# Two batches' softmax in another order: the first one finished first, its transpose in halves, one power for both norms

## The chip, the cores and the metric

The kernel runs on one core of a Trainium2 chip. The metric is the device time of one execution in microseconds (us): the median of several runs. PE is the matrix engine (TensorE), PEld its weight loads, DVE the VectorE, ACT the ScalarE, POOL the GpSimd, SP the engine that issues nearly all DMAs.

## The reference

For 64 batches of 128 tokens and 512 features, x gets a residual added: multi-query attention with 16 heads of width 64, one key and one value shared by all heads, between two layernorms. All of it is fp32.

```python
xn = layernorm(x, g_in)
q = (xn @ Wq).reshape(b, n, H, DH).transpose(0, 2, 1, 3) * DH ** (-0.5)
kv = xn @ Wkv                       # k, v: 64 columns each, shared by the heads
# a null key and a null value (from cond) stand ahead of the 128 others
sim = einsum('bhid,bjd->bhij', q, k) + bias
sim = where(causal or masked, -max, sim)
attn = softmax(sim)
out = einsum('bhij,bjd->bhid', attn, v).reshape(b, n, H * DH) @ Wo
x = x + layernorm(out, g_out)
```

## The kernel before, in words

Every engine executes its instructions in the order in which the Python program issues them (a manual schedule); an instruction waits for the results, and for the buffers, that it needs. So the order of the calls in the step functions is the order on each engine, and there is no planner.

The 64 batches are handled as 32 pairs. Step `d` has a first part, `turn_full(d)`, and a second, `body_full(d)`; the steps 4 to 29 use these two, the first and last steps have functions of their own. In step `d` four jobs are under way at once:

- the **softmax** of the batches `a = 2d` and `b = 2d + 1`;
- the **output** of the pair before, `p = 2d - 2`: probabilities times values (`values`), then the product with Wo (`out_product`, seven products of a Strassen scheme, with sums of the inputs by `out_sum` on POOL);
- the **last norm** and the store of the pair before that, `l = 2d - 4`;
- for the group of four batches to come, `g = d // 2 + 1`: q, by an outer and an inner Strassen scheme (`product_two`, `inner_products` on PE, and `inner_out`, which adds inner products from PSUM into `qT` on DVE), k and v (`kv_pair`, `kv_pair_out`), and for the group after it the first norm of two batches `m` and `m + 1` of x.

A step with even `d` (`h = 0`, "even step" below) also has `token_sums_inner` on POOL; a step with odd `d` ("odd step") transposes the values (`values_T`) and starts the sums of the next group (`next_sums`, POOL).

The scores of a batch are an array `s` of 128 partitions by 8 rows by 194 columns. It has a lower part (`hf = 0`, 64 keys) and an upper part (`hf = 1`, 128 keys), each normalized by itself because the rows are different queries. Per batch and part:

- `scores_max`, DVE, L831: negative row maxima, `nmax`;
- `exps`, ACT, L840: one exponential for each of the 8 rows, with the row sum taken along (each has a second instruction that reads the accumulator);
- `rinv`, DVE, L858: reciprocals of the sums;
- `scale`, POOL, L862: the part times the reciprocals.

When both parts of a batch are scaled, `blocks_T` (DVE, L878) transposes the whole in blocks of 32 by 32 into `sb`, from which `values` reads in the next step. `bias_add` (POOL, L764) writes bias plus mask into the `s` of a coming batch. There are three buffers for `s`, so `bias_add(b + 2)` writes where batch `a` was and waits for the transpose of `a`.

The inner products of q have four outputs, `pi2`, `pi3`, `pi7` and `pi4` in the trace's names (the trace merges them as `pi`). Each takes seven small matmuls whose sums build up in three PSUM regions. PE may only overwrite or add to a region after DVE's `inner_out` (L744) has read its state: PE and DVE hand each other the same tile several times a step. `out_keep(p, "X", "yu2")` (DVE, L1055) is such a hand-over for the output product in `pyX`: it copies product 6's state before product 7 adds to it.

The norms: `two_stats` (L316 to L321) takes statistics of two tiles on DVE and a power of -1/2 on POOL (`pow`), and `two_nmr` (L327) makes -mean/std from them on DVE. `norm_apply` (ACT, L358) and `pair_norm` (ACT, L1092) apply the norm to x and to the output; `tokens_T` (L382) transposes the normalized x; `pair_gain` (L1095) and `pair_residual` (L1098) finish an output, `store` sends it.

Of the kernel before, what the change touches and what calls it, by code (L numbers as in the profile page):

```python
# [17 lines left out]
def kernel(  # L18
# [63 lines left out]
    P = 128  # L82
# [223 lines left out]
        nc.gpsimd.tensor_tensor(rstd, rstd, nhalf, ALU.pow)  # L306
        stats[m] = mv, rstd

    def two_stats(tiles, name):

        mv = small.tile([P, 2, 2], FP, tag=f"mv{name}", name=f"mv{name}")
        rstd = small.tile([P, 2], FP, tag=f"rs{name}", name=f"rs{name}")
        sts = []
        for t in tiles:
            st = small.tile([P, 6], FP, tag="st", name="st")
            nc.vector.bn_stats(st, t)  # L316
            sts.append(st)
        for i, st in enumerate(sts):
            nc.vector.bn_aggr(mv[:, i], st)
        nc.vector.tensor_scalar(rstd, mv[:, :, 1], EPS, None, ALU.add)  # L320
        nc.gpsimd.tensor_tensor(rstd, rstd, nhalf.broadcast_to([P, 2]), ALU.pow)  # L321
        return mv, rstd

    def two_nmr(mv, rstd, name):
        nmr = small.tile([P, 2], FP, tag=f"nm{name}", name=f"nm{name}")
        for i in range(2):
# [8 lines left out]
        return [(nmr[:, i : i + 1], rstd[:, i : i + 1]) for i in range(2)]  # L335

    xnmr = {}

# [812 lines left out]
    def turn_full(d):  # L1151

        a, b, p = 2 * d, 2 * d + 1, 2 * d - 2
        g, h = d // 2 + 1, d % 2
        home = lower_rooms(a)
        scores(a, 0, home=home[0])
        scores(b, 0, home=home[1])
        scores(a, 1)
        scores(b, 1, ((ps_y, "X"), (ps_q, "c")))
        scores_add(a, 0)  # L1160
        scores_add(b, 0)
        scores_max(a, 0)
# [12 lines left out]
        exps(a, 0)  # L1175
        keep_two("a", g, h, "p1")
        scores_max(b, 0)
        rinv(a, 0)
        scale(a, 0)
        exps(b, 0, 0, 3)  # L1180
        values_out(p, po)
        step_home(d)

    def next_sums(g):

        for k in (1, 2, 3):
            token_sum(g, k)
        token_sums_inner(g, 2)
# [255 lines left out]
    def body(d):  # L1444
# [20 lines left out]
        if h == 1:  # L1465
            load_mask(g + 1)
        if ln:
            nmrs[l], nmrs[l + 1] = two_nmr(*on, "o")
        xn = two_stats((xs[m], xs[m + 1]), "x")
        scores_max(a, 1)  # L1470
        product(g, f0, 1, ps_q, "a")
        keep("a", g, f0, "p1")
# [7 lines left out]
            product(g, f0, 2, ps_w, "w")  # L1480
            q_out(g, f0, 0, "w", "p1")
        scores_max(b, 1)
        xnmr[m], xnmr[m + 1] = two_nmr(*xn, "x")
        if ln:
            pair_gain(l)
            pair_residual(l)
# [105 lines left out]
    def body_full(d):  # L1592
# [3 lines left out]
        xw = g + 1 < NG  # L1596
        m = (g + 1) * GB + 2 * h
        sums = h == 0
        if sums:
            token_sums_inner(g, 7)  # L1600
        if xw:
            xn = two_stats((xs[m], xs[m + 1]), "x")
        on = two_stats((ys[l], ys[l + 1]), "o")
        pkv = kv_pair(g * GB + 2 * h, (ps_q, "c"))
        if xw:
            xnmr[m], xnmr[m + 1] = two_nmr(*xn, "x")
        nmrs[l], nmrs[l + 1] = two_nmr(*on, "o")
        scores_max(a, 1)
        kv_pair_out(g * GB + 2 * h, pkv)
        if h == 1 and xw:  # L1610
            load_mask(g + 1)
        if xw:
            norm_apply(m)
            norm_apply(m + 1)
        product_two(g, h, 6, ps_q, "a", start=False)
        inner_room(2, g, h)
        inner_products(2, g, h, (1,))
        out_sum(p, 0)
        if sums:
            token_sum(g, 4)  # L1620
        out_product(p, 1, ps_y, "X")
        out_sum(p, 1)
        out_sum(p, 2)
        if xw:
            tokens_T(m)
            tokens_T(m + 1)
            if h == 1:
                tokens_out(g + 1)
        pair_norm(l)
        inner_out(2, g, h, "00")  # L1630
        keep_two("a", g, h, "u2")
        scores_max(b, 1)
        out_keep(p, "X", "yp1")
        pair_norm(l + 1, (ps_y, "Y"))
        product_two(g, h, 5, ps_q, "c")
        exps(b, 0, 3)
        pair_gain(l)
        pair_residual(l)
        store(l)
        pair_gain(l + 1)  # L1640
        inner_products(2, g, h, (6,))
        inner_out(2, g, h, "01")
        if sums:
# [13 lines left out]
        if sums:  # L1657
            token_sums_inner(g, 4)
# [12 lines left out]
        out_product(p, 5, ps_y, "Y")  # L1671
        exps(a, 1, 2)
        if not sums:
            scale(b, 0)
        rinv(a, 1)
        scale(a, 1)
        if sums:
            scale(b, 0)
# [18 lines left out]
        if h == 1:  # L1697
            values_T(g)
# [213 lines left out]
```

## Time and profile before

| | |
|---|---|
| time, median of 3 runs | 1085.35 us (1085.19 to 1085.71) |
| the profiled execution: time / span | 1085.17 us / 1083.4 us |
| mean granted TensorE clock | 0.998 |
| busy, share of the span | PE 95%, PEld 83%, DVE 83%, POOL 74%, ACT 61% |
| HBM | 63.19 MB read, 33.55 MB written |

The time of the profiled execution is 1.8 us above its span; the rest of the text compares with this execution. How to read the rows:

- A timeline row has the start and the duration in us, the engine, the line and operation, `out<-in` by the program's names, the shape, the number of instructions merged (x2), and in brackets how long the engine had been idle and whose result ended that.
- A row of the waits reads "engine line <- engine line it waited for: us in total, times, longest us".
- A row of the stages has the window in us, its length, and the busy us (and instructions) of PE, PEld, DVE, ACT and POOL, then the granted clock, the DMA share and GB/s.
- A row of the groups has the number of instructions after x, then busy us and mean ns of one, then idle us before them.

### The profile page before, as it was taken

Reading aid. Unit: us, or ns where it says so; the run is one execution under the profiler, and the core shown is the slowest. Engines: PE = TensorE matmul, PEld = TensorE weight load, DVE = VectorE, ACT = ScalarE, POOL = GpSimd, SP = SyncE. Lnnn points to the kernel's source line nnn. Section 1 sums busy time; section 2 is a strip of 40 time slices with the busy share of each in tenths; the row PEclk is TensorE's granted clock in tenths of the full one; section 3 lists DMA queues with packets and bytes.
Section 4 is the critical chain, followed back from the end, with each engine's and each line's share of the span. In section 5 each row is a group of like instructions: output and inputs, shape, how many; then the busy total and the mean of one; then the engine's idle time right before and its main releaser. Section 6 shows DMA issues by size and latency. Waiting matters only on the chain.

```text
span 1083.4 us, 32419 instructions
## 1 busy us (share of the span) xinstructions
PE 1034.0 (95%) x12805; PEld 901.4 (83%) x12805; DVE 897.4 (83%) x1954; ACT 661.9 (61%) x2675; POOL 798.6 (74%) x676
## 2 busy tenths in 40 slices
PE   9999999999999999999999999999999999999997
PEld 8888878878888788888888888888887888888886
DVE  6867778888888888888888888888888888887787
ACT  4766657755567555676555775556765557745483
POOL 4998588596785967759677595776868768686676
PEclk9999999999999999999999999999999999999999
DMA  7415242421524215152241522415224152321211
GB/s 207 133 30 140 65 131 73 123 70 60 145 62 125 84 46 149 55 137 75 68 139 42 146 72 86 114 42 147 79 90 103 42 160 68 99 72 41 86 61 59
DMA packets 73839, 100.92 MB, mean 93 GB/s; under 512 B 32212, under 2 KB 36056, under 8 KB 71896
## 3 DMA queue, kind: packets, MB, share of 16 engines
q1 hardware_dynamic: 73392, 98.47, 30.8%
q8 instruction: 100, 1.64, 0.6%
q14 instruction: 51, 0.42, 0.1%
q10 hardware_dynamic: 296, 0.40, 0.1%
HBM read 63.19 MB, written 33.55 MB: 89 GB/s over the span
## 4 chain that ended last, share of the span: by engine, by line
PE 59%; POOL 22%; DVE 14%; issue 4%; ACT 1%; DMA 0%; POOLq 0%; DVEq 0%
PE pi L716 11%; PE pyX L1028 10%; PE pyY L1028 7%; POOL s L764 7%; PE pa L618 5%; POOL xS L561 4%; PE po L939 4%; PE pkv L419 3%; POOL xI L695 3%; POOL s L862 3%; DVE sb L878 3%; PE pyw L1028 3%; DVE qT L744 3%; PE pq L514 3%; DVE nmax L831 3%
## 5 line engine op out<-in xcount | busy, mean ns | idle before, releaser
L840 ACT ACTIVATE s<-s,nmax 128x65 f32<-128x65 f32 (+1 forms) x1024 | 371.2, 369 | 78.4 <-DVE nmax L831 78.3
L862 POOL TENSOR_TENSOR s<-s,rinv 128x512 f32<-128x512 f32 (+1 forms) x132 | 190.1, 1446 | 143.3 <-DVE rinv L858 143.0
L764 POOL TENSOR_TENSOR s<-biasp,mneg 128x1552 f32<-128x1552 f32 (+1 forms) x65 | 206.1, 3173 | 45.1 <-ACT mneg L751 39.9
L744 DVE TENSOR_TENSOR qT<-pi,qT 128x128 f32<-128x128 f32 (+1 forms) x480 | 161.1, 345 | 62.5 <-PE pi L716 57.1
L840 ACT ACTIVATION_READ_ACCUMULATOR s<-s,nmax 128x1 f32 x1024 | 197.8, 193 | 0.0
L1064 ACT COPY y<-pyX 128x256 f32<-128x256 f32 x29 | 10.8, 373 | 249.3 <-PE pyX L1028 249.3
L831 DVE TENSOR_REDUCE nmax<-s 128x8 f32<-128x1032 f32 (+1 forms) x128 | 121.8, 952 | 0.1
L878 DVE STREAM_TRANSPOSE sb<-s 128x1536 f32<-128x1536 f32 (+1 forms) x68 | 112.4, 1657 | 3.6 <-POOL s L862 3.6
L1028 PE MATMUL pyX<-wT,oT 128*128 128x256 f32 x464 | 109.8, 380 | 0.0
L1028 PE MATMUL pyX<-wo,oT 128*128 128x256 f32 x464 | 109.8, 380 | 0.0
L1008 POOL TENSOR_TENSOR oT<-oT 128x512 f32<-128x512 f32 x64 | 81.4, 1274 | 15.0 <-PE pyw L1028 12.8
L1028 PEld LDWEIGHTS pyX<-wT,oT 128*128 128x128 f32 x464 | 84.2, 191 | 9.1
L1028 PEld LDWEIGHTS pyX<-wo,oT 128*128 128x128 f32 x464 | 84.2, 191 | 9.0
L939 PE MATMUL po<-sb,vr 32*64 32x128 f32 (+1 forms) x3232 | 83.5, 301 | 0.5 <-DVE s L824 0.4
L939 PEld LDWEIGHTS po<-sb,vr 32*64 32x64 f32 x3232 | 71.6, 130 | 14.0 <-issue 9.1
L716 PE MATMUL pi<-xS,wq 128*128 128x128 f32 x260 | 55.6, 296 | 26.5 <-DVE qT L744 26.5
L716 PEld LDWEIGHTS pi<-xS,wq 128*128 128x128 f32 x260 | 41.2, 190 | 41.6 <-DVE qT L744 36.9
L939 PE MATMUL po_s<-sb,vr 32*64 32x128 f32 (+1 forms) x864 | 65.3, 302 | 1.0 <-DVE s L826 1.0
L419 PE MATMUL pkv<-xT,wkv 128*128 128x256 f32 x256 | 63.3, 391 | 0.0
L958 ACT ACTIVATE oT<-po,nv 128x512 f32<-128x512 f32 (+1 forms) x101 | 61.6, 654 | 0.6 <-POOL s L764 0.6
L1028 PE MATMUL pyY<-wo,oT 128*128 128x256 f32 x256 | 60.6, 380 | 0.0
L1028 PE MATMUL pyw<-wo,oT 128*128 128x256 f32 x256 | 60.5, 380 | 0.0
(243 smaller groups left out, 2690.7 us busy)
## 6 DMA issues: line engine op xcount, KB each, us to landing
out_dram<-y SPq DMA_DIRECT2D x63, 256.0 KB
x<-in_x_dram SPq DMA_DIRECT2D x62, 256.0 KB
xd<-xb SPq DMA_DIRECT2D x14, 1024.0 KB
xT<-xd SPq DMA_DIRECT2D x56, 256.0 KB
home<-in_x_dram SPq DMA_DIRECT2D x56, 256.0 KB
vr<-vd SPq DMA_DIRECT2D x64, 128.0 KB
kT<-kT SPq DMA_DIRECT2D x32, 64.0 KB
vd<-vb SPq DMA_DIRECT2D x32, 64.0 KB
```

The source lines that it names most:

```text
L419: nc.tensor.matmul(pkv, wkv[:, kc, :], xT[g][:, t : t + 2, kc, :], start=(kc == 0), stop=(kc == KC - 1),)
L716: nc.tensor.matmul(to, inner_w[k][i][:, h], inner_x[k, g][i], start=(i == 1), stop=True, skip_group_check=(i != 1),)
L744: nc.vector.tensor_tensor(o, p, o, ALU.add)
L764: nc.gpsimd.tensor_tensor(S[b][:, :, keys], biasp[:, :, keys], mneg[:, t, keys] .unsqueeze(1) .broadcast_to([P, R8, keys.stop - keys.start ...
L831: nc.vector.tensor_reduce(nmax[b][:, hf], S[b][:, :, WITH_NULL[hf]], AX.X, ALU.max, negate=True)
L840: nc.scalar.activation(row, row, AF.Exp, bias=nmax[b][:, hf, k : k + 1], accum_out=rsum[b][:, hf, k : k + 1],)
L862: nc.gpsimd.tensor_tensor(sv, sv, rinvs[b, hf][:, lo:hi].unsqueeze(2).broadcast_to([P, hi - lo, sv.shape[2]]), ALU.mult,)
L878: nc.vector.transpose(sbs[b][:, :, lo:hi].rearrange("p j e q -> p e j q"), S[b][:, lo:hi, 1 : ROW - 1].rearrange("p e (j k) -> p e j k", k=Q),
L939: nc.tensor.matmul(po[s][rows, to : to + n], vr[g][quad, t, PLACE[j], :], sb[quad, slots, r * NF : (r + 1) * NF, :], start=(turn == 0), st ...
L958: nc.scalar.activation(to, src, AF.Identity, bias=nv2)
L1008: eng.tensor_tensor(o, a, b, op)
L1028: nc.tensor.matmul(prod[key], h[:, c, :], w[:, c, :], start=(start and c == 0), stop=(c == HC - 1), skip_group_check=not start,)
```

## The change

Lines of the changed program are two to four higher than before for the same operation (L744 is L746, L862 is L864, L878 is L880). The change is in `body_full`, but for the norm helpers and one line of `turn_full` that concerns step 4 alone.

- **Exponentials.** Before: 5 lower ones of `b` (three were done in the first part of the step), 8 upper ones of `a`, 8 upper ones of `b`. Now: 8 upper ones of `a`, 5 lower of `b`, 8 upper of `b`. `rinv(a, 1)` and `scale(a, 1)` move ahead of `rinv(b, 0)` and `scale(b, 0)`.
- **Transposes.** `blocks_T(a)` and `blocks_T(b)` become two halves each (`lo`: rows 0 to 3, `hi`: rows 4 to 7). Those of `a` stand among the reads of `pi7`, `pi3` and `pi2`, ahead of where the whole one stood. Those of `b` stand ahead of and behind the last reads of `pi4`. `scale(b, 1)` is cut likewise.
- **`bias_add(b + 2)`** goes ahead of `scale(b, 1)` on POOL. In step 29 the one for the last batch goes with it.
- **Norms.** `stats_of` takes the four tiles (two of x, two of the output) in one go with one power, and `nmr_of` makes the four results after it; `scores_max(a, 1)` stands between.
- **Order on DVE besides.** `tokens_T`, the first read of `pi2` and the gains come earlier, `scores_max(b, 1)` and `values_T` later.

```diff
+    def stats_of(tiles, name):
+        n = len(tiles)
...
         nc.vector.tensor_scalar(rstd, mv[:, :, 1], EPS, None, ALU.add)
-        nc.gpsimd.tensor_tensor(rstd, rstd, nhalf.broadcast_to([P, 2]), ALU.pow)
+        nc.gpsimd.tensor_tensor(rstd, rstd, nhalf.broadcast_to([P, n]), ALU.pow)
...
     def turn_full(d):
         if d == 4:
-            next_sums(g)
+            token_sum(g, 1)
+            token_sum(g, 2)
...
     def body_full(d):
-        if xw:
-            xn = two_stats((xs[m], xs[m + 1]), "x")
-        on = two_stats((ys[l], ys[l + 1]), "o")
+        tiles = [ys[l], ys[l + 1]]
+        if xw:
+            tiles = [xs[m], xs[m + 1], *tiles]
+        n4 = stats_of(tiles, "n")
+        scores_max(a, 1)
         pkv = kv_pair(g * GB + 2 * h, (ps_q, "c"))
+        nm = nmr_of(*n4, "n")
...
-        scores_max(a, 1)
         kv_pair_out(g * GB + 2 * h, pkv)
...
-        scores_max(b, 1)
         out_keep(p, "X", "yp1")
-        exps(b, 0, 3)
...
         pair_gain(l + 1)
+        exps(a, 1)
         inner_products(2, g, h, (6,))
...
+        scores_max(b, 1)
         out_product(p, 2, ps_w, "w")
...
-        rinv(b, 0)
-        exps(a, 1, 0, 2)
         keep_two("a", g, h, "u3")
+        rinv(a, 1)
+        scale(a, 1)
         inner_products(2, g, h, (7, 5, 2))
         inner_out(2, g, h, "11")
         inner_out(2, g, h, "00,11")
+        exps(b, 0, 3)
...
+        rinv(b, 0)
+        scale(b, 0)
+        blocks_T(a, *lo)
         out_product(p, 5, ps_y, "Y")
-        exps(a, 1, 2)
...
+        exps(b, 1, 0, 2)
         inner_products(7, g, h, (6,))
         inner_out(7, g, h, "01")
+        out_keep(p, "Y", "yp5")
+        exps(b, 1, 2)
...
         q_out_two(g, h, 1, 1, "c", "u3")
+        blocks_T(a, *hi)
         inner_products(2, g, h, (4, 3))
         inner_out(2, g, h, "01,10")
-        exps(b, 1, 0, 4)
-        out_keep(p, "Y", "yp5")
-        exps(b, 1, 4)
+        bias_add(b + 2)
+        if d == PAIRS - 3:
+            bias_add(B - 1)
...
         rinv(b, 1)
-        blocks_T(a)
-        scale(b, 1)
-        bias_add(b + 2)
-        if d == PAIRS - 3:
-            bias_add(B - 1)
+        scale(b, 1, *lo)
+        scale(b, 1, *hi)
         if h == 1 and xw:
             next_sums(g + 1)
         inner_products(4, g, h, (6,))
         inner_out(4, g, h, "01")
+        if h == 1:
+            values_T(g)
         out_product(p, 7, ps_y, "X", start=False)
         out_part(p + 1, 1, "X")
+        blocks_T(b, *lo)
         inner_products(4, g, h, (7, 5, 2))
...
-        blocks_T(b)
+        blocks_T(b, *hi)
         out_product(p, 4, ps_y, "X", start=False)
```

PE's order and SP's order of DMAs stay as they were. The order on POOL in the odd step 15 (batches `a` = 30 and `b` = 31), from the output sums to the next group's sums, before:

```order
L1008 TENSOR_TENSOR oT_28_6557<-oT_28_6557 128x512 x2
L862 TENSOR_TENSOR s_31_6351<-s_31_6351,rinv_31_0_6667 128x8x64
L862 TENSOR_TENSOR s_30_6135<-s_30_6135,rinv_30_1_6698 128x8x128
L862 TENSOR_TENSOR s_31_6351<-s_31_6351,rinv_31_1_6748 128x8x128
L764 TENSOR_TENSOR s_33_6753<-biasp_86,mneg_118 128x1552
L561 TENSOR_TENSOR xS1_9_6755<-xT_9_6651 128x512
```

The same stretch of POOL now, where `s_33` is the buffer of `s_30`:

```order
L1010 TENSOR_TENSOR oT_28_6535<-oT_28_6535 128x512 x2
L864 TENSOR_TENSOR s_30_6115<-s_30_6115,rinv_30_1_6648 128x8x128
L864 TENSOR_TENSOR s_31_6310<-s_31_6310,rinv_31_0_6666 128x8x64
L766 TENSOR_TENSOR s_33_6700<-biasp_86,mneg_118 128x1552
L864 TENSOR_TENSOR s_31_6310<-s_31_6310,rinv_31_1_6716 128x4x128 x2
L563 TENSOR_TENSOR xS1_9_6720<-xT_9_6626 128x512
```

Batch 30 is scaled first, and the bias of batch 33 stands ahead of the last scaling of batch 31, which is in two. On DVE in the same step, the end from the last reciprocal on, before (`pi4` and `pyX` are PE's, `sb` the transposes):

```order
L858 RECIPROCAL rinv_31_1_6748<-rsum_31_6553 128x8
L878 STREAM_TRANSPOSE sb_30_6750<-s_30_6135 128x8x6x32
L744 TENSOR_TENSOR qT_8_1_0_6459<-pi4_8_1_6728,qT_8_1_0_6459 128x2x64
L1062 TENSOR_TENSOR y_29_6718<-pyX_28_1_6613,y_29_6718 128x256
L744 TENSOR_TENSOR qT_8_1_0_6459<-pi4_8_1_6728,qT_8_1_0_6459 128x2x64
L744 TENSOR_TENSOR qT_8_1_0_6459<-pi4_8_1_6728,qT_8_1_0_6459 128x2x2x64
L636 TENSOR_TENSOR qT_8_1_1_6460<-pc_8_1_5_6633,qT_8_1_1_6460 128x8x64
L1062 TENSOR_TENSOR y_28_6629<-pyY_28_5_6686,y_28_6629 128x256
L744 TENSOR_TENSOR qT_8_1_0_6459<-pi4_8_1_6728,qT_8_1_0_6459 128x4x64
L878 STREAM_TRANSPOSE sb_31_6786<-s_31_6351 128x8x6x32
```

The same end on DVE now:

```order
L860 RECIPROCAL rinv_31_1_6716<-rsum_31_6531 128x8
L746 TENSOR_TENSOR qT_8_1_0_6437<-pi4_8_1_6706,qT_8_1_0_6437 128x2x64
L459 STREAM_TRANSPOSE vb_8_6732<-vT_8_6176 64x512
L1064 TENSOR_TENSOR y_29_6680<-pyX_28_1_6591,y_29_6680 128x256
L880 STREAM_TRANSPOSE sb_31_6747<-s_31_6310 128x4x6x32
L746 TENSOR_TENSOR qT_8_1_0_6437<-pi4_8_1_6706,qT_8_1_0_6437 128x2x64
L746 TENSOR_TENSOR qT_8_1_0_6437<-pi4_8_1_6706,qT_8_1_0_6437 128x2x2x64
L638 TENSOR_TENSOR qT_8_1_1_6438<-pc_8_1_5_6606,qT_8_1_1_6438 128x8x64
L1064 TENSOR_TENSOR y_28_6601<-pyY_28_5_6671,y_28_6601 128x256
L746 TENSOR_TENSOR qT_8_1_0_6437<-pi4_8_1_6706,qT_8_1_0_6437 128x4x64
L880 STREAM_TRANSPOSE sb_31_6747<-s_31_6310 128x4x6x32
```

The transpose of batch 30 no longer stands between the last reciprocal and the second read of `pi4`; the first half of batch 31's now stands ahead of the third and fourth reads.

In the stretch of DVE before these, from the first reads of `pi3` to its last read, the order before was:

```order
L744 TENSOR_TENSOR qT_8_1_1_6460<-pi3_8_1_6683,qT_8_1_1_6460 128x2x64
L744 TENSOR_TENSOR qT_8_1_0_6459<-pi7_8_1_6671,qT_8_1_0_6459 128x4x64
L744 TENSOR_TENSOR qT_8_1_0_6459<-pi7_8_1_6671,qT_8_1_0_6459 128x2x2x64
L636 TENSOR_TENSOR qT_8_1_1_6460<-pc_8_1_5_6633,qT_8_1_0_6459 128x8x64
L744 TENSOR_TENSOR qT_8_1_0_6459<-pi2_8_1_6610,qT_8_1_0_6459 128x4x64
L744 TENSOR_TENSOR qT_8_1_0_6459<-pi4_8_1_6728,qT_8_1_0_6459 128x2x64
L1055 COPY y_28_6629<-pyX_28_1_6613 128x256
```

And now, with the first half of batch 30's transpose ahead of it:

```order
L860 RECIPROCAL rinv_31_0_6666<-rsum_31_6531 128x8
L880 STREAM_TRANSPOSE sb_30_6669<-s_30_6115 128x4x6x32
L746 TENSOR_TENSOR qT_8_1_0_6437<-pi7_8_1_6643,qT_8_1_0_6437 128x2x64
L746 TENSOR_TENSOR qT_8_1_1_6438<-pi3_8_1_6663,qT_8_1_1_6438 128x2x64
L746 TENSOR_TENSOR qT_8_1_0_6437<-pi7_8_1_6643,qT_8_1_0_6437 128x4x64
L746 TENSOR_TENSOR qT_8_1_0_6437<-pi7_8_1_6643,qT_8_1_0_6437 128x2x2x64
L638 TENSOR_TENSOR qT_8_1_1_6438<-pc_8_1_5_6606,qT_8_1_0_6437 128x8x64
L880 STREAM_TRANSPOSE sb_30_6669<-s_30_6115 128x4x6x32
L746 TENSOR_TENSOR qT_8_1_0_6437<-pi2_8_1_6587,qT_8_1_0_6437 128x4x64
L746 TENSOR_TENSOR qT_8_1_0_6437<-pi4_8_1_6706,qT_8_1_0_6437 128x2x64
L1057 COPY y_28_6601<-pyX_28_1_6591 128x256
```

Both halves of batch 30 now stand on DVE ahead of the first read of `pi4` and the copy from `pyX`.

More of the change, by code (lines that the diff above doesn't have):

```diff
@@ L320, in two_stats, with nmr_of @@
         nc.vector.tensor_scalar(rstd, mv[:, :, 1], EPS, None, ALU.add)
-        nc.gpsimd.tensor_tensor(rstd, rstd, nhalf.broadcast_to([P, 2]), ALU.pow)
+        nc.gpsimd.tensor_tensor(rstd, rstd, nhalf.broadcast_to([P, n]), ALU.pow)
         return mv, rstd
-    def two_nmr(mv, rstd, name):
-        nmr = small.tile([P, 2], FP, tag=f"nm{name}", name=f"nm{name}")
-        for i in range(2):
+    def nmr_of(mv, rstd, name):
+        n = rstd.shape[1]
+        nmr = small.tile([P, n], FP, tag=f"nm{name}", name=f"nm{name}")
+        for i in range(n):
             nc.vector.tensor_scalar(
@@ L334, in two_nmr @@
             )
-        return [(nmr[:, i : i + 1], rstd[:, i : i + 1]) for i in range(2)]
+        return [(nmr[:, i : i + 1], rstd[:, i : i + 1]) for i in range(n)]
     xnmr = {}
@@ L1598, in body_full @@
         sums = h == 0
[L1599 removed]
+        lo, hi = (0, R8 // 2), (R8 // 2, R8)
+        if d == 4:
+            token_sums_inner(g, 2)
+        elif sums:
             token_sums_inner(g, 7)
+        tiles = [ys[l], ys[l + 1]]
         if xw:
[L1602 to L1603 removed]
+            tiles = [xs[m], xs[m + 1], *tiles]
+        n4 = stats_of(tiles, "n")
+        scores_max(a, 1)
         pkv = kv_pair(g * GB + 2 * h, (ps_q, "c"))
+        nm = nmr_of(*n4, "n")
+        nmrs[l], nmrs[l + 1] = nm[-2:]
         if xw:
[L1606 to L1608 removed]
+            xnmr[m], xnmr[m + 1] = nm[:2]
         kv_pair_out(g * GB + 2 * h, pkv)
@@ L1617, in body_full @@
         inner_products(2, g, h, (1,))
+        inner_out(2, g, h, "00")
         out_sum(p, 0)
+        if d == 4:
+            token_sum(g, 3)
+            token_sums_inner(g, 7)
         if sums:
@@ L1639, in body_full @@
         store(l)
+        product_two(g, h, 5, ps_q, "c")
+        pair_norm(l + 1, (ps_y, "Y"))
         pair_gain(l + 1)
+        exps(a, 1)
         inner_products(2, g, h, (6,))
@@ L1670, in body_full @@
         inner_out(3, g, h, "00")
-        out_product(p, 5, ps_y, "Y")
-        exps(a, 1, 2)
[L1673 to L1678, printed above, removed]
+        if sums:
+            token_sums_inner(g, 4)
+        rinv(b, 0)
+        scale(b, 0)
+        blocks_T(a, *lo)
+        out_product(p, 5, ps_y, "Y")
+        exps(b, 1, 0, 2)
         inner_products(7, g, h, (6,))
         inner_out(7, g, h, "01")
+        out_keep(p, "Y", "yp5")
+        exps(b, 1, 2)
         inner_products(3, g, h, (6, 5))
```

26 lines of the change are left out of this document (10 added, 16 removed).

## The prediction, as it was put on record

> **What bounds the kernel now.** I read the page first, its busy times and the chain that ended last:
>
> ```profile
> PE 1034.0 (95%) x12805; PEld 901.4 (83%) x12805; DVE 897.4 (83%) x1954; ACT 661.9 (61%) x2675; POOL 798.6 (74%) x676
> PE 59%; POOL 22%; DVE 14%; issue 4%; ACT 1%; DMA 0%; POOLq 0%; DVEq 0%
> ```
>
> PE is the bound, but the chain leaves it for 36% of the span. Next the stages: step 14 (even, from 492.08) and step 15 (odd, from 525.64). Then the waits of the whole run:
>
> ```profile
> 492.08:525.64 33.56, 31.97 (x401) 27.67 (x401) 28.29 (x63) 20.05 (x81) 28.71 (x29) 1.00 0.22 66
> 525.64:558.83 33.19, 31.70 (x401) 27.82 (x400) 28.28 (x64) 20.87 (x83) 20.15 (x14) 1.00 0.43 121
> PE pi L716 <- DVE qT L744: 30.2, 38, 1.5
> PE pc L618 <- DVE vT L446: 8.1, 12, 0.7
> ```
>
> PE's own work in a pair of steps is 63.7 us of 66.75, so 3.1 us a pair are idle, and nearly all of it is waiting for DVE: 38.3 us in the run. More than that no order of the other engines can bring. The clock is 1.00 throughout. The timeline of the odd step's end shows the largest of these waits:
>
> ```profile
> 550.72 1.89 PE L1028 MATMUL pyX<-wo,oT 128*128 128x256 f32 x8
> 552.11 1.73 DVE L878 STREAM_TRANSPOSE sb<-s 128x1536 f32<-128x1536 f32 x1
> 552.27 1.90 POOL L862 TENSOR_TENSOR s<-s,rinv 128x1024 f32<-128x1024 f32 x1 [4.23 <-DVE rinv L858]
> 553.76 0.25 DVE L744 TENSOR_TENSOR qT<-pi,qT 128x128 f32<-128x128 f32 x1
> 554.06 0.49 PE L716 MATMUL pi<-xS,wq 128*128 128x128 f32 x2 [1.45 <-DVE qT L744]
> 554.13 3.22 POOL L764 TENSOR_TENSOR s<-biasp,mneg 128x1552 f32<-128x1552 f32 x1
> 557.01 1.89 PE L1028 MATMUL pyX<-wT,oT 128*128 128x256 f32 x8
> ```
>
> The transpose of `a` holds DVE for 1.73 us, the read of `pi4` (553.76) stands behind it, and PE waits 1.45 us. POOL had been idle for 4.23 us.
>
> **The change part by part.** PE's instructions are unchanged, so the sum is where PE's last output product of a step (557.01) comes to stand. I walk the step with these prices:
>
> ```profile
> L878 DVE STREAM_TRANSPOSE sb<-s 128x1536 f32<-128x1536 f32 x60 | 105.0, 1750 | 3.6 <-POOL s L862 3.6
> L878 DVE STREAM_TRANSPOSE sb<-s 128x768 f32<-128x768 f32 x8 | 7.4, 956 | 0.0
> L862 POOL TENSOR_TENSOR s<-s,rinv 128x512 f32<-128x512 f32 x72 | 75.4, 1050 | 28.3 <-DVE rinv L858 28.3
> L321 POOL TENSOR_TENSOR rso<-rso,nhalf 128x2 f32<-128x2 f32 x28 | 19.3, 691 | 12.4 <-DVE rso L320 12.4
> ```
>
> Half a transpose is 0.956 us, so a cut costs 0.16 us of DVE, 0.32 a step. On DVE the next instruction starts 0.08 us before the one ahead ends (552.11 to 553.76 is 1.65 for 1.73), so I take 0.88 for a half in a queue. A cut `scale` is twice 1.05 for 1.90.
>
> [...] With nothing overlapped a half would take its 0.956 in the queue, and by that the sum below would be some 0.24 us a step worse, about 1085 us in all; the 1.65 above speaks for the overlap.
>
> The odd step's beginning and middle:
>
> ```profile
> 531.88 1.24 DVE L316 BATCH_NORM_STATS2 st<-x 128x6 f32<-128x512 f32 x2
> 536.02 1.54 ACT L358 ACTIVATE x<-x,nmx,rsx 128x512 f32<-128x512 f32 x2
> 538.87 0.82 ACT L1092 ACTIVATE yn<-y,nmo,rso 128x512 f32<-128x512 f32 x1
> 1005.49 0.34 ACT L840 ACTIVATE s<-s,nmax 128x65 f32<-128x65 f32 x1
> 1007.16 0.39 ACT L840 ACTIVATE s<-s,nmax 128x129 f32<-128x129 f32 x1
> 542.29 1.27 POOL L1008 TENSOR_TENSOR oT<-oT 128x512 f32<-128x512 f32 x1 [0.99 <-PE pyw L1028]
> 546.31 0.29 DVE L744 TENSOR_TENSOR qT<-pi,qT 128x128 f32<-128x128 f32 x1 [0.26 <-PE pi L716]
> 546.66 0.49 PE L716 MATMUL pi<-xS,wq 128*128 128x128 f32 x2
> 547.41 0.89 DVE L744 TENSOR_TENSOR qT<-pi,qT 128x256 f32<-128x256 f32 x2 [0.35 <-PE pi L716]
> 548.33 0.69 DVE L636 TENSOR_TENSOR qT<-pc,qT 128x512 f32<-128x512 f32 x1
> 548.93 0.41 DVE L744 TENSOR_TENSOR qT<-pi,qT 128x256 f32<-128x256 f32 x1
> 550.01 0.41 DVE L1055 COPY y<-pyX 128x256 f32<-128x256 f32 x1
> ```
>
> *Norms.* Four statistics in one go take DVE from 531.88 to about 534.9 (2.3 us, four short aggregates, one sum). Then comes `scores_max(a, 1)`, some 1.2 us, to 536.1. The one power, for which I take 0.7 to 1 us from the 0.691 of two values, is done beneath it; without that cover it would cost what is left of it. x is normalized from 536.4, 0.4 later than at 536.02. Behind it on ACT wait both `pair_norm` and the exponentials.
>
> *Exponentials.* ACT's second `pair_norm` then ends at 538.87 + 0.82 + 0.4 = 540.1. Eight upper ones at 0.385 give 543.15; a copy of some 0.6, 543.7; five lower ones in 1007.16 - 1005.49 = 1.67, 545.4. `rinv(b, 0)` is done at 545.6. POOL has the last sum at 542.29 + 1.27 = 543.56 and, with 1.90, `scale(a, 1)` at 545.5.
>
> *First half of `a`.* It starts at 545.65, now ahead of the read at 546.31, which moves to 545.65 + 0.88 = 546.53. PE, which waits for that read, goes on at 546.87 instead of 546.66: a new wait, 0.2 lost.
>
> *Second half.* By the spacings of the rows (0.75 from PE to the read of `pi7`, 0.92, 0.60) it runs from 549.14 to 550.10. Read of `pi2` (0.33), first read of `pi4` (0.21) and the copy from `pyX` follow, which ends at 550.97 instead of 550.42; product 7 starts at 551.0, 0.28 late. After it PE meets no transpose: the wait of 1.45 goes.
>
> *What is late next.* POOL may start `bias_add(b + 2)` at 550.15: 3.22 to 553.37; half a scale, 554.45; first half of `b`, 554.5 to 555.38 in the queue; two reads of `pi4`, to 556.0. For these PE waits at its last inner products, some 0.9 us, and the last output product starts 0.55 later, at 556.6 instead of 557.01: **-0.4 us an odd step**. The second halves lie beside PE's last product. `values_T` is later by some 1.5 us with its DMAs; its values are read a step later, and nothing else on SP moves past them. The stores and the tokens' transfer come earlier.
>
> The even step:
>
> ```profile
> 503.08 1.89 PE L1028 MATMUL pyX<-wo,oT 128*128 128x256 f32 x8
> 506.00 1.27 POOL L1008 TENSOR_TENSOR oT<-home,oT 128x512 f32<-128x512 f32 x1
> 510.34 1.28 POOL L1008 TENSOR_TENSOR oT<-oT 128x512 f32<-128x512 f32 x1
> 514.33 0.49 PE L716 MATMUL pi<-xS,wq 128*128 128x128 f32 x2
> 523.82 1.46 PE L1028 MATMUL pyX<-wT,oT 128*128 128x256 f32 x6
> ```
>
> Here POOL is the late one. With one power fewer and the next group's sums started earlier it reaches the sum at 506.00 as soon as product 1 ends, 504.97, so 1.0 earlier; the last sum ends at 510.6, `scale(a, 1)` at 512.5, the first half of `a` frees DVE at 513.46, and PE goes on at 513.8 instead of 514.33. The wait of `pc` for `vT` (0.7) has gone on the way. From here it is the odd step's chain, 9.75 from 546.87 to 556.6: 523.55 instead of 523.82, **-0.3**.
>
> Step 29 differs: two biases stand ahead of `scale(b, 1)`.
>
> ```profile
> 1008.23 1.27 POOL L1008 TENSOR_TENSOR oT<-oT 128x512 f32<-128x512 f32 x1 [0.98 <-PE pyw L1028]
> 1012.26 0.49 PE L716 MATMUL pi<-xS,wq 128*128 128x128 f32 x2
> 1019.74 6.37 POOL L764 TENSOR_TENSOR s<-biasp,mneg 128x1552 f32<-128x1552 f32 x2
> 1022.61 1.89 PE L1028 MATMUL pyX<-wT,oT 128*128 128x256 f32 x8
> ```
>
> `scale(a, 1)` ends at 1011.4, PE goes on at 1012.67, the second half ends 3.23 later, at 1015.9; 6.37 of bias, 1.05 of scale, 0.88 of transpose and 0.6 of reads bring PE's last product to 1025.5 instead of 1022.61: **+2.9**. Step 4 has two POOL sums fewer ahead and gets them back later; -2 to +1, taken as 0.
>
> Sum: 12 pairs of steps (4 to 27) at -0.7 are -8.4; step 28 -0.3; step 29 +2.9: -5.8. The profiled execution took 1085.17 us (0.18 below the median), so **1079.4 us**. The unknown prices (four powers, overlap, the copy) move a step by 0.3 either way, 8 us in all.
>
> **The rivals.**
>
> *The chain through POOL is longer than walked.* In the new order everything from `scale(a, 1)` to PE's last product is one series: half, hand-overs, half, bias, scale, half, reads. Each us by which the second half of `a` ends later is a us of the step. From 5.8 / 25 = 0.23 us a step the change is slower than before; at 0.7 it is -5.8 + 25 x 0.7, 1097 us. For it: the bias alone is 3.22, and before it lay behind the last scale. Against: POOL idled 4.23 at that place. Chance 0.27.
>
> *The hand-overs go better.* If half of the 3 us idle in a pair go, 12 x 1.5 less 2.9 gives 1070; all of it, 1052. For it: I used upper values for ACT. Chance 0.15.
>
> *The waits only change place*, 1085, chance 0.07.
>
> *A lock.* Now every half stands beside a scale, a sum or a bias on POOL. If the two excluded each other, each half would wait for the POOL instruction under way, some 1.5 us a step over two or three halves: -5.8 + 25 x 1.5, 1117 us. Rows 552.11 and 552.27 ran at the same time at usual length, 60 transposes average 1.75. Chance 0.03. [...]
>
> **How the numbers follow.** The forecast has 0.48, the better case 0.15: faster by over 0.2% (2.2 us, about what a measurement can tell from no change) 0.63. Same 0.07, slower 0.30. The range runs from the middle of the better case (between 1070 and 1052) to just past the slower one's price, 1063 to 1098; outside it are about 0.05 of the better case, 0.10 of the slower one and the lock.
>
> **What would show it.** Right: PE's 1.45 us wait behind the transpose is gone, PE waits at the first half of `a` and at the last `pi4` products for under 1 us each, steps of 32.8 and 33.3 us, step 29 near 36. Wrong: a PE wait of over 1.3 us for the reads behind `b`'s first half, POOL's bias ending past 554, or DVE waiting for `scale(a, 1)` beyond 546.

## The result, and the profile after

The changed kernel takes 1087.56 us (median of 20 runs, 1086.61 to 1089.71), the kernel before 1085.37 us (20 runs, 1084.83 to 1086.84): ratio 1.0022, 95% interval 1.0015 to 1.0029. It is slower by 0.2%, where 1079.4 us was forecast. Its profiled execution took 1087.89 us, 2.72 more than that of before. The mean granted clock of its 20 executions lies between 0.992, which the profiled one has, and 0.997.

The page of the changed kernel, busy times and the chain that ended last:

```profile
PE 1034.5 (95%) x12805; PEld 906.9 (83%) x12805; DVE 882.2 (81%) x1982; ACT 662.0 (61%) x2675; POOL 794.3 (73%) x678
PE 44%; POOL 27%; DVE 23%; issue 4%; ACT 1%; DMA 0%; POOLq 0%; DVEq 0%
```

PE's share of the chain fell from 59 to 44%, and POOL and DVE together have 50% of it instead of 36%: more of the chain goes through hand-overs between POOL, DVE and PE.

Steady steps first: step 14 (from 493.11) and step 15 (from 526.51), in one stretch each:

```profile
493.10:526.50 33.40, 31.61 (x401) 27.80 (x400) 27.45 (x63) 19.94 (x81) 27.00 (x28) 1.00 0.22 66
526.50:559.20 32.70, 31.69 (x401) 27.82 (x400) 27.88 (x64) 20.95 (x83) 21.45 (x15) 1.00 0.44 125
```

PE's waits in their second parts, and its last output product in each, from its timeline (in brackets the idle time ahead and what ended it):

```profile
514.86 0.49 PE L718 MATMUL pi<-xS,wq 128*128 128x128 f32 x2 [1.00 <-DVE qT L746]
524.17 0.46 PE L718 MATMUL pi<-xI,wq 128*128 128x128 f32 x2 [0.79 <-DVE qT L746]
524.69 1.89 PE L1030 MATMUL pyX<-wT,oT 128*128 128x256 f32 x8
547.53 0.49 PE L718 MATMUL pi<-xS,wq 128*128 128x128 f32 x2 [0.28 <-DVE qT L746]
556.85 0.49 PE L718 MATMUL pi<-xI,wq 128*128 128x128 f32 x2 [0.73 <-DVE qT L746]
557.40 1.89 PE L1030 MATMUL pyX<-wT,oT 128*128 128x256 f32 x8
```

The wait of 1.45 us is gone. In its place stand a wait at the first half of `a` and one at the last products of `pi4`, both at most 1.01 us in all steady steps. These steps became shorter, so the loss must be elsewhere. I took the time from the first score product (`sc_w`) of a step to that of the next, from the timelines:

| step | before | after | difference |
|---|---|---|---|
| 4 | 35.49 | 39.26 | +3.77 |
| 5 to 27, all | 767.36 | 760.08 | -7.28 |
| of these an odd one / an even one (median) | 33.19 / 33.55 | 32.69 / 33.42 | -0.50 / -0.13 |
| 28 | 32.30 | 33.40 | +1.10 |
| 29 | 32.85 | 38.03 | +5.18 |

The gain of 7.3 us is there, and three steps at the edges of the loop lose 10.05. Step 4, rows of POOL, DVE and PE in order of time:

```profile
165.50 1.05 POOL L864 TENSOR_TENSOR s<-s,rinv 128x512 f32<-128x512 f32 x1 [2.58 <-DVE rinv L860]
180.67 1.90 POOL L864 TENSOR_TENSOR s<-s,rinv 128x1024 f32<-128x1024 f32 x1
182.60 0.98 DVE L880 STREAM_TRANSPOSE sb<-s 128x768 f32<-128x768 f32 x1 [2.49 <-POOL s L864]
183.81 0.49 PE L718 MATMUL pi<-xS,wq 128*128 128x128 f32 x2 [2.72 <-DVE qT L746]
184.81 3.17 PE L1030 MATMUL pyX<-wT,oT 128*128 128x256 f32 x8
```

The same place in stretches of 2 us; the third number from the end is the granted clock:

```profile
184.00:186.00 2.00, 2.00 (x12) 1.84 (x12) 1.37 (x3) 0.00 (x0) 1.46 (x2) 0.81 0.02 7
186.00:188.00 2.00, 2.00 (x7) 1.57 (x6) 1.36 (x3) 0.00 (x0) 0.87 (x1) 0.50 0.00 0
```

POOL idles 2.58 us before `scale(a, 0)`, since the sums that stood there before were moved behind it, and comes to `scale(a, 1)` only at 180.67. DVE waits for that with the first half of `a`, and PE waits 2.72 us for the read behind it. Then the clock falls to half, and eight products take 3.17 us instead of 1.89. Three runs below (`bias29`, `fill29`, `fill29b`) have step 4 in the same order: in their profiles PE's wait at this place is 4.09 us, and the step takes 40.40, 39.30 and 40.10 us. In the profile shown here PE comes to the wait 1.4 us later, after its clock had been low once before in this step (0.69 in the stretch from 164 to 166 us, 0.50 from 166 to 168), with no wait over 0.98 us ahead of that.

Step 29, the same engines:

```profile
1013.82 6.35 POOL L766 TENSOR_TENSOR s<-biasp,mneg 128x1552 f32<-128x1552 f32 x2 [3.53 <-DVE sb L880]
1020.13 2.04 POOL L864 TENSOR_TENSOR s<-s,rinv 128x512 f32<-128x512 f32 x2
1021.21 0.98 DVE L880 STREAM_TRANSPOSE sb<-s 128x768 f32<-128x768 f32 x1 [4.12 <-POOL s L864]
1022.88 0.79 PE L718 MATMUL pi<-xI,wq 128*128 128x128 f32 x2 [3.85 <-DVE qT L746]
1023.89 3.62 PE L1030 MATMUL pyX<-wT,oT 128*128 128x256 f32 x8
```

```profile
1022.00:1024.00 2.00, 1.12 (x5) 1.12 (x6) 1.72 (x5) 0.00 (x0) 0.18 (x1) 0.50 0.95 311
1024.00:1026.00 2.00, 2.00 (x6) 1.58 (x6) 1.79 (x5) 0.00 (x0) 0.35 (x1) 0.50 0.74 268
```

The two biases end at 1020.13, the scale, the half and the reads follow in a row, PE waits 3.85 us, and here too its next products run at half clock (the two stretches). The waits of PE for DVE's reads in the whole run:

```profile
PE pi L718 <- DVE qT L746: 40.5, 51, 3.9
```

That is 10 us more than before (30.2): the two long waits alone are 6.6 us, and in steps 5 to 27 these waits rose from 27.3 to 31.8 us. PE's waits for `vT` (8.1 us before) are gone instead. By the stage rows, PE's idle time fell in step 15 (1.49 to 1.01 us) but rose in step 14 (1.59 to 1.79). The even step is shorter all the same because PE's busy time fell, from 31.97 to 31.61 us for the same 401 instructions. It has two waits in it now instead of three; what made the 0.36 us, no run here takes apart.

### The profile page after: what moved, and what is told of

It reads as the page before. It is cut to its first block, busy times and chain, and to the rows that moved or that the text cites. A ratio compares the mean times of both kernels' runs of the same rounds, so it can differ in the third digit from the quotient of the medians.

```text
span 1086.1 us, 32474 instructions
## 1 busy us (share of the span) xinstructions
PE 1034.5 (95%) x12805; PEld 906.9 (83%) x12805; DVE 882.2 (81%) x1982; ACT 662.0 (61%) x2675; POOL 794.3 (73%) x678
## 3 DMA queue, kind: packets, MB, share of 16 engines
HBM read 63.19 MB, written 33.55 MB: 89 GB/s over the span
## 4 chain that ended last, share of the span: by engine, by line
PE 44%; POOL 27%; DVE 23%; issue 4%; ACT 1%; DMA 0%; POOLq 0%; DVEq 0%
PE pyX L1030 8%; DVE sb L880 7%; POOL s L864 7%; POOL oT L1010 7%; POOL s L766 6%; PE pa L620 5%; PE pi L718 4%; DVE qT L746 4%; PE po L941 4%; PE pkv L421 3%; DVE s L826 3%; DVE st L317 3%; PE pq L516 3%; PE pyw L1030 3%; PE sc_Y L811 3%
## 5 line engine op out<-in xcount | busy, mean ns | idle before, releaser
L864 POOL TENSOR_TENSOR s<-s,rinv 128x512 f32<-128x512 f32 (+1 forms) x158 | 194.2, 1238 | 47.0 <-DVE rinv L860 46.3
L746 DVE TENSOR_TENSOR qT<-pi,qT 128x128 f32<-128x128 f32 (+1 forms) x480 | 152.7, 335 | 33.6 <-PE pi L718 29.2
L880 DVE STREAM_TRANSPOSE sb<-s 128x768 f32<-128x768 f32 (+1 forms) x120 | 122.8, 1025 | 42.3 <-POOL s L864 41.5
L1030 PE MATMUL pyX<-wT,oT 128*128 128x256 f32 x464 | 112.8, 387 | 0.0
L718 PE MATMUL pi<-xS,wq 128*128 128x128 f32 x260 | 53.0, 286 | 18.4 <-DVE qT L746 18.4
L718 PEld LDWEIGHTS pi<-xS,wq 128*128 128x128 f32 x260 | 43.6, 191 | 26.2 <-DVE qT L746 23.4
L826 DVE TENSOR_TENSOR s<-sc_w,s 128x256 f32<-128x256 f32 x64 | 26.8, 419 | 45.4 <-PE sc_w L811 43.5
```

What stands on the lines that cost most here:

```text
L718: nc.tensor.matmul(to, inner_w[k][i][:, h], inner_x[k, g][i], start=(i == 1), stop=True, skip_group_check=(i != 1),)
L746: nc.vector.tensor_tensor(o, p, o, ALU.add)
L864: nc.gpsimd.tensor_tensor(sv, sv, rinvs[b, hf][:, lo:hi].unsqueeze(2).broadcast_to([P, hi - lo, sv.shape[2]]), ALU.mult,)
L880: nc.vector.transpose(sbs[b][:, :, lo:hi].rearrange("p j e q -> p e j q"), S[b][:, lo:hi, 1 : ROW - 1].rearrange("p e (j k) -> p e j k", k=Q),
L1030: nc.tensor.matmul(prod[key], h[:, c, :], w[:, c, :], start=(start and c == 0), stop=(c == HC - 1), skip_group_check=not start,)
```

## The experiments

The theory: the new order gains in the steady steps, and the loss lies in the order of POOL's work in steps 4, 28 and 29, with a lower clock behind the long waits of PE (0.50 behind 2.72 and 3.85 us). The rival: the new order does not suit these steps, or their neighbours make them late, so that no single place of POOL's work is to blame.

**`sums4`: step 4's sums back ahead of the first scale.**

```diff
 # turn_full, d == 4
-            token_sum(g, 1)
-            token_sum(g, 2)
+            next_sums(g)        # sums 1, 2, 3 and the inner sums 2
 # body_full: inner sums 2 first and sum 3 later go; inner sums 7 first, as in other even steps
```

> Step 4's sums only (token_sum 3 and the inner sums 2) go back to the place they had before, ahead of scale(a, 0), all else as changed. Theory A (PE waits in step 4 because POOL does these sums between the output sums and so comes late to scale(a, 1)): POOL uses its 2.6 us idle ahead of scale(a, 0), scale(a, 1) starts near 178 instead of 180.7, PE's wait of 2.72 us falls under 0.5, the slow clock behind it goes, step 4 takes 35 to 36 us instead of 39.3, total near 1083.5. Rival B (step 4 loses because the new order as such doesn't suit it): the step stays over 38 us and the total near 1087.5.

1083.66 us (11 runs; the kernel before, measured beside it, 1085.38; ratio 0.9985, 0.9976 to 0.9993). Its timeline in step 4, POOL's scale and PE's wait:

```profile
177.94 1.91 POOL L864 TENSOR_TENSOR s<-s,rinv 128x1024 f32<-128x1024 f32 x1
181.08 0.49 PE L718 MATMUL pi<-xS,wq 128*128 128x128 f32 x2 [1.15 <-DVE qT L746]
```

The scale is 2.7 us earlier, the step takes 35.90 us instead of 39.26, and the clock stays at 1.00 there. PE's wait fell to 1.15 and not below 0.5: 1.00 is what every even step of this order has. Theory A holds. The total says less than the step: in this profile step 29, whose order is as changed, takes 36.78 us instead of 38.03, with the clock at 0.50 for half as long.

**`bias29`: the last batch's bias ahead of the other one, in step 29.**

```diff
         rinv(b, 0)
         scale(b, 0)
+        if d == PAIRS - 3:
+            bias_add(B - 1)
         blocks_T(a, *lo)
 ...
         bias_add(b + 2)
-        if d == PAIRS - 3:
-            bias_add(B - 1)
```

> In step 29 alone, the last batch's bias (its tile is not one of the three that rotate) stands behind scale(b, 0), where POOL idles 3.5 us, instead of behind bias_add(b + 2). Theory A (the second bias holds scale(b, 1) up, and the PE wait of 3.85 us lowers the granted clock): scale(b, 1) starts near 1017 instead of 1020.1, PE's wait falls to 0.8, no slow clock, step 29 takes 33.2 instead of 38.0 us, total near 1082.7. Rival B (the step is late for another reason, a wait of POOL or the clock by itself): the step gains under 1 us, or only the 3.2 us of the bias without the 1.7 of the clock, 1084.4.

1083.12 us (11 runs; ratio 0.9979, 0.9970 to 0.9987). Step 29 takes 32.69 us, 5.34 less. POOL's two biases and PE's wait:

```profile
1011.48 3.21 POOL L766 TENSOR_TENSOR s<-biasp,mneg 128x1552 f32<-128x1552 f32 x1
1015.04 3.20 POOL L766 TENSOR_TENSOR s<-biasp,mneg 128x1552 f32<-128x1552 f32 x1 [0.36 <-DVE sb L880]
1020.95 0.49 PE L718 MATMUL pi<-xI,wq 128*128 128x128 f32 x2 [0.70 <-DVE qT L746]
```

The first of them now lies in time in which POOL idled (3.53 us). PE's wait is 0.70 us, the clock stays at 1.00 there, and the step gains more than the 3.2 us of the bias: theory A. (Step 4 has its own fall of the clock in this profile, 40.40 us for 39.26.) This one line, in this one step, turns the changed kernel from slower than the kernel before to 0.2% faster.

**`fill29`, `fill29b`: needless products in PE's long wait.** Both leave the order of step 29 as changed; the edit shown is that of `fill29b`.

```diff
         if d == PAIRS - 3:
+            room = ps_q.tile([P, 2, HT], FP, tag="a", name="fill")
+            for _ in range(8):
+                nc.tensor.matmul(room[:, 0], wq[:, 0, 0:P],
+                                 operands(g, 5)[1][:, :, 0, :], start=True, stop=True)
         inner_products(4, g, h, (4, 3))
```

> Step 29's order stays as changed, but PE does 16 needless products (3.5 us, into a PSUM bank that nobody reads) in its wait of 3.85 us. Theory A (the granted clock falls because PE had nothing to do): the clock stays at 1.00, PE's last output product takes 1.9 instead of 3.6 us, step 29 takes 36.3 instead of 38.0, total near 1085.8, although PE does more. Rival B (the clock falls for another reason, by time or by load): the step takes 38.0 or more, total 1087.5 or above.

> The changed kernel, and in step 29 PE does 8 needless products (16 passes of 0.22 us, 3.5 us in all) into a PSUM room that is free by then, ahead of the last products of pi4, so that it is busy while POOL does its two biases. Theory A (the granted clock falls because PE has nothing to do for 3.85 us): the wait falls to about 0.3 us, the clock stays at 1.00, PE's last output product takes 1.9 instead of 3.6 us, step 29 takes 36.3 instead of 38.0 us, total near 1085.8. Rival B (the clock falls for another reason): the clock is at 0.5 there all the same, step 29 takes 38.0 us or more.

`fill29` missed its aim: written into the other half of `pi4`'s room, its products waited with `pi4` (3.86 us, as before) and then took 8.77 us; 1094.22 us tells nothing on the question. `fill29b` uses a room of its own. PE's rows, and the clock in a stretch of 2 us:

```profile
1019.78 3.62 PE L1733 MATMUL fill<-xS,wq 128*128 128x256 f32 x16
1023.81 0.49 PE L718 MATMUL pi<-xI,wq 128*128 128x128 f32 x2 [0.41 <-DVE qT L746]
1024.36 1.89 PE L1030 MATMUL pyX<-wT,oT 128*128 128x256 f32 x8
```

```profile
1024.00:1026.00 2.00, 2.00 (x12) 1.69 (x11) 1.93 (x7) 0.00 (x0) 0.00 (x0) 1.00 0.66 223
```

With more to do PE is sooner done: clock 1.00, 1.89 us, step 29 35.85 us, 2.18 less. PE goes on with `pi4` as long after the step's start as without the filling (33.47 us and 33.46), so all of the gain is the clock's. So the clock fell in this step because PE had nothing to do. The total (1087.51 us, forecast 1085.8) did not follow: in this profile step 30 takes 19.84 us instead of 18.23 (PE stands idle there for 0.54 and 0.77 us without anything in the profile that it waits for), and step 4, which has its own fall of the clock, 40.10 instead of 39.26. Why step 30 takes longer stays open.

**`old3`: steps 4, 28 and 29 with the old body.**

```diff
-            body_full(d)
+            body_old(d) if d in (4, 28, 29) else body_full(d)   # and next_sums(g) in step 4
```

> The old body (with its two norms, whole transposes and old order) in steps 4, 28 and 29 alone, the new one in steps 5 to 27. Theory A (the steady steps gain 0.63 us a pair and all the loss sits in these three steps): 35.5, 32.3 and 32.9 us as before there, 10 us less than the changed kernel, 1077.5. Rival B (the edges lose because of what the new steps beside them hand over): these steps take over 1 us longer than before, total 1080 to 1085.

1078.37 us (5 runs; ratio 0.9933, 0.9919 to 0.9946), steps 4, 28 and 29 at 35.52, 31.99 and 32.86 us, steps 5 to 27 at 760.1 as in the changed kernel. The two parts of the account stand apart, as theory A has it. The next four runs change one part of the new body in steps 5 to 27 of `old3`, so their times compare with 1078.37.

**`even_scale`: the late scale of the even step.**

```diff
-        out_sum(p, 3)
+        if not sums:
+            out_sum(p, 3)
 ...
         scale(a, 1)
+        if sums:
+            out_sum(p, 3)
```

> As old3 (old body in steps 4, 28, 29), and in the even steps of the new body scale(a, 1) stands ahead of the last output sum (out_sum 3) on POOL instead of behind it. Theory A (in the even step POOL reaches scale(a, 1) 1.2 us too late, so PE waits 1.00 us there, and this wait eats most of the gain): the wait falls to 0 to 0.3 us, even steps take 32.5 to 32.7 us instead of 33.42, 11 of them give 8 to 10 us, total 1068 to 1071. Rival B (the even step is bound elsewhere, by the later part of the chain or by the output sum that is now later): even steps stay within 0.2 us of 33.42 and the total near 1078.

1069.19 us (4 runs; ratio 0.9852, 0.9837 to 0.9867); even steps 32.65 us instead of 33.41, odd ones unchanged. PE's wait in step 14:

```profile
506.99 0.49 PE L718 MATMUL pi<-xS,wq 128*128 128x128 f32 x2 [0.24 <-DVE qT L746]
```

So the even step's gain had stopped at 0.13 us because of one sum that POOL did first.

**`whole_T`: no cut.**

```diff
-        blocks_T(a, *lo)          # and of b
+        blocks_T(a)
 ...
-        blocks_T(a, *hi)
-        scale(b, 1, *lo)
-        scale(b, 1, *hi)
+        scale(b, 1)
```

> As old3, and in the new body both transposes are whole again, each at the place of its first half (scale(b, 1) whole too); all else in the new order. Theory A (the cut lets DVE take its reads in between, which is worth more than its 0.3 us of DVE): the reads behind stand 0.85 us later at both places, steps take 0.4 to 0.9 us more, total 1087 to 1098. Rival B (the cut costs only its fixed part and the order alone brings the gain, the bias being free earlier): steps 0 to 0.3 us shorter, total 1072 to 1078.

1095.53 us (4 runs; ratio 1.0097, 1.0084 to 1.0111); odd steps 33.35 (+0.66), even ones 34.15 (+0.74). PE waits 1.81 us in even steps and 1.08 in odd ones for the read behind the transpose of `a`, instead of 1.00 and 0.28: theory A. The cut, with the later place that it allows for the second halves, is worth 0.7 us a step; without it the new order is slower than the kernel before.

**`two_pow`: the norms apart.**

```diff
-        n4 = stats_of(tiles, "n")
+        if xw:
+            xn = stats_of((xs[m], xs[m + 1]), "x")
+        on = stats_of((ys[l], ys[l + 1]), "o")
```

> As old3, and in the new body the norms are apart again (two powers of 0.7 us instead of one of 1.02, two sums on DVE), else the new order. Theory A (POOL is late in the even step, so its 0.38 us more is paid there, and in the odd step it lies in POOL's idle time): even steps +0.3 to +0.4 us, odd steps 0 to +0.1, total 1081.5 to 1084. Rival B (the power is hidden in both): within 0.5 us of 1078.4.

1079.10 us (5 runs); even steps 33.47 (+0.06), odd ones 32.70 (+0.01). Rival B: the shared power brings next to nothing. From the start of `scale(a, 0)` to that of `scale(a, 1)` in step 14, POOL takes 12.26 us (497.59 to 509.85) against 12.21 in the changed kernel (499.50 to 511.71): of the 0.37 us that two powers take more (0.70 and 0.69 for 1.02), most goes into gaps of some 0.1 us between POOL's instructions, one of them ahead of the power, where POOL waited for the statistics.

**`bias_late`: the bias behind `scale(b, 1)`.**

```diff
-        bias_add(b + 2)
 ...
         scale(b, 1, *hi)
+        bias_add(b + 2)
```

> As old3, and in the new body bias_add(b + 2) stands behind scale(b, 1) again, as in the kernel before. Theory A (the bias ahead of the scale makes PE's wait of 0.73 to 0.79 us at the last products of pi4, but it uses POOL's idle time, which is lost otherwise): that wait goes, 0.5 to 0.7 us an odd step, but POOL begins the even step some 1.6 us later, where it is the late one: pairs between -0.3 and +0.8 us, total 1075 to 1088. Rival B (the bias ahead of the scale is a plain loss): both steps 0.6 us shorter, total near 1064. Rival C (the early bias is what the whole gain rests on): pairs back to 66.7 us, total 1086 or more.

1073.79 us (4 runs; ratio 0.9895, 0.9881 to 0.9908); odd steps 31.72 (-0.97), even ones 34.00 (+0.59), and step 28, though it has the old body, 33.37 instead of 31.99. Theory A, a little beyond the good end of its range (1075 us for the total, -0.3 for a pair; measured -0.38): the bias ahead of the scale costs the step that it stands in, and a late one costs the step behind it if POOL is the late one there. That holds for even steps, whose sums POOL begins at the end of the odd one; the odd step begins with POOL idle. The +0.59 is a net, since the even steps' own bias is late here too. Step 28 shows the price by itself: with the old body, only the late bias of step 27 is new ahead of it, and it takes 1.38 us more.

**`best`: these findings together.**

```diff
 # new body in steps 5 to 29; even_scale's order; in step 29 bias_add(B - 1) behind scale(b, 0)
+        late = sums or d == PAIRS - 3
+        if not late:
+            bias_add(b + 2)
         ...
         scale(b, 1, *hi)
+        if late:
+            bias_add(b + 2)
```

> What the runs so far point to, put together: the new body in steps 5 to 29, scale(a, 1) ahead of the last output sum in even steps, bias_add(b + 2) behind scale(b, 1) in even steps and in step 29 (the odd step begins with POOL idle, so a late bias costs nothing there) and ahead of it in the other odd steps, the last batch's bias behind scale(b, 0) in step 29, the old body in step 4. Theory A (the waits add as the single runs showed): even steps 31.8 us instead of 32.65, odd ones 32.69, steps 28 and 29 31.8 each, total 1057 to 1060. Rival B (a late bias in an even step makes the odd step's first scale late): odd steps 33 or more, total 1064 to 1070.

1056.04 us (4 runs, 1055.30 to 1056.25; the kernel before, measured beside it, 1085.61): ratio 0.9726, 0.9712 to 0.9739, 2.7% faster than the kernel before. Even steps take 31.62 us, odd ones 32.70, steps 28 and 29 31.46 and 31.71. That is theory A, and a little better than its 1057 to 1060; the odd steps did not become longer. The busy times of its page, and PE's wait for the reads in the whole run:

```profile
PE 1026.2 (97%) x12805; PEld 902.8 (86%) x12805; DVE 880.1 (84%) x1981; ACT 661.8 (63%) x2675; POOL 795.2 (75%) x678
```

```profile
PE pi L718 <- DVE qT L746: 15.7, 38, 0.7
```

PE waits 15.7 us for the reads, against 40.5 in the changed kernel (its longest 3.9) and 30.2 before.

**`lock4`: two sums on DVE at another place.**

```diff
 # end of body(3)
-            weight_sums_inner(4, (3,))
-            weight_sums_inner(7, (3,))
 # turn_full, behind scale(a, 0)
+        if d == 4:
+            weight_sums_inner(4, (3,))
+            weight_sums_inner(7, (3,))
```

> As old3, and the two last sums of inner weights (both inputs and the output in SBUF) stand on DVE in step 4 behind scale(a, 0), beside short sums of POOL, instead of at the end of step 3, beside the bias of 3.2 us. Theory A (such a sum on DVE waits until POOL's instruction under way has ended): they take under 1.5 us each instead of 0.84 and 3.43, the first addition of scores in step 4 starts 2 us sooner, step 4 takes 33.5 to 35.2 instead of 35.5 us (POOL may bind then). Rival B (the sum takes 3.4 us for a reason of its own, its operands or PE's reads): it takes over 2.5 us there too, step 4 the same or longer.

1078.72 us (4 runs), as `old3`. The kernel before, all sums of this line from `wq` to `wq` on DVE (shortest, median and longest in ns, then first and last start), and the bias on POOL beside the last of them:

```profile
L673 DVE TENSOR_TENSOR wq<-wq x3: 420/843/3432, 81.8 to 156.8; 128x256 f32<-128x256 f32 x3
```

```profile
156.51 3.40 POOL L764 TENSOR_TENSOR s<-biasp,mneg 128x1552 f32<-128x1552 f32 x1
```

The same sums in `lock4`, and PE's wait in its step 4:

```profile
L675 DVE TENSOR_TENSOR wq<-wq x3: 418/946/1191, 82.2 to 164.2; 128x256 f32<-128x256 f32 x3
```

```profile
172.30 1.99 PE L620 MATMUL pc<-xS,wS 128*128 128x256 f32 x8 [2.57 <-DVE vT L448]
```

The same sum takes 0.42 us alone, 3.43 beside the bias (it ends 0.3 us after the bias) and under 1.2 beside short sums of POOL. Theory A on the duration. The time is not won: the first addition of scores is 2 us earlier, but PE then waits 2.57 us for `vT`, and step 4 takes 35.44 us instead of 35.52.

## Why the prediction was wrong

Against the sum of -5.8 us the profiled executions differ by +2.72. Of the 8.5 us between, step 4 makes 4.1, step 29 2.3, step 28 1.4 and the steady steps 0.8.

**The steady steps: right.** Step 15 starts 0.87 us later than before, step 14 1.03 later; less that, PE goes on behind the first half at 546.66 (546.87 forecast) and 513.83 (513.8), and the last product starts at 556.53 (556.6) and 523.66 (523.55). The new waits of 0.28 and 0.73 us in the odd step were given as 0.2 and 0.9. Odd steps gained 0.50 (0.4 forecast), even ones 0.13 (0.3): the even step's term was a little too good, since its chain from PE's restart is 9.83 us and not 9.75, and its length moved less than its last product (-0.16). Steps 5 to 27 at -7.28 stand against -8.1 forecast (12 x 0.4 + 11 x 0.3). That PE's own work in a pair (63.7 us) is fixed was not quite so: it fell by 0.36 us in the even step.

**Step 4, "taken as 0": wrong, +3.77.** The step that failed is that I gave it bounds of -2 to +1 and did not walk it. (The sum even has it at -0.3, as one of the 12 pairs from 4 to 27.) I had noted that it "has two POOL sums fewer ahead and gets them back later", and that POOL is the late one of an even step. The two belong together: work taken out of POOL's idle time (2.58 us) and put into its queue ahead of the scale is paid in full: `scale(a, 1)` came 2.7 us later for it. `sums4` gives 3.36 us of the step back, the slow products behind the wait with them.

**Step 28, -0.3: wrong, +1.10.** I gave it an even step's price and never looked at its own length. It was 32.30 us before, not 33.55, as no norm of x is left there; in the new order it is bound like any even step: PE waits 1.00 us at the same place, and the step takes 33.40. With the old body it takes 31.99.

**Step 29, +2.9: the chain was right and its term still too small, +5.18.** By PE's last product it is 1023.89, plus the 2.18 us by which the step starts earlier (its first `sc_w` at 989.42 for 991.60), 1026.07 for 1022.61: +3.46, of which some 0.4 is already PE at half clock; the rest is that last product itself, 3.62 us for 1.89. `fill29b` measures the clock's part by itself: 2.18 us, so 3.0 are left for the chain, which the walk had at 2.9. The size of the clock's part changes: with the same order the step took 36.78 us in the profile of `sums4`. A clock of 0.50 at PE waits of 2.72 and 3.85 us was in no term and no rival; the trace of before, whose longest wait of this kind was 1.5 us, does not show it: its clock was 1.00 in every stretch of 2 us from 40 to 1078 us.

**The rivals.** The chain through POOL was not longer than walked in the steady steps, so the slower time came by a way that no rival had. The lock was given to transposes; the halves took 0.98 us (the median) beside POOL, so that was rightly set aside. Waits that only change place (1085) was the nearest in time, by another mechanism. The range's lower end, said to be the middle of 1070 and 1052, would be 1061 and not 1063; nothing hangs on it.

**The parts of the change.** Of the gain, the cut carries the most (without it +0.7 us a step), the shared power next to nothing (`two_pow`, +0.7 us in all), and the early bias costs the step that it stands in about 1 us: 0.97 in an odd one (`bias_late`), 1.03 in an even one (`best`: 31.62 us for 32.65, the odd steps behind it unchanged). In an odd step it also saves time in the even step behind it, 1.38 us for step 28 of `bias_late`. The orders of the exponentials and of the two batches' scales were not taken back alone.

## What to carry to other kernels

Walk the first and the last passage of a loop by their own rows, above all where a condition on the step adds or leaves out work: here 23 steps gained 7 us and three lost 10. For work on an engine that is late, ask in which of its idle times it lies now, and where it will lie: the same bias, scale or sum is free in one step and costs time in the next, so even and odd steps may want different orders. At PE's waits of 2.72 and 3.85 us here the output product behind took 3.17 and 3.62 us for 1.89: such a wait has to be priced with the products behind it.

## What the runs showed of the hardware

**The clock behind a wait.** At PE waits of 2.72 (step 4) and 3.85 us (step 29) the granted clock was 0.50 for 3.4 and 6.8 us (worked out from the shares in stretches of 2 us; in step 29 this begins within the wait, with 0.88 from 1020 to 1022 us), and products took up to 1.9 times as long (3.62 us for 1.89); keeping PE busy in step 29 kept it at 1.00 there (`fill29b`). Which waits have this behind them, these runs do not settle: the wait of 2.57 us in `lock4` left the clock at 1.00, while in `whole_T` one wait of 1.81 us, as in its other even steps, was followed by 0.50, and that step alone took 35.82 us instead of 34.15. The first fall in step 4 of the changed kernel had no wait over 0.98 us ahead of it; in `even_scale`, which has one at the same place (0.57 from 164 to 168 us), step 4 took 35.66 us against 35.52 in `old3`, whose clock was 1.00 there, so this fall came with 0.14 us.

**A sum on DVE beside POOL's bias.** DVE's sum from `wq` to `wq`, with both inputs in SBUF, took 3.43 us beside POOL's bias and ended 0.3 us after it, for 0.42 alone, in both kernels alike. `yn<-yn,gob`, with one input in PSUM (0.69 us beside a sum of POOL in step 15, and at most 0.70 in the whole run), and the transposes (0.98 us for a half beside POOL's scale in step 15) did not wait so. What sets the one apart from the others, no run here takes apart.
